# Block maxima of a context taken ahead of its keys and values, and gates loaded later, in the opening stage of a two-layer gated cross-attention kernel

## The chip, the cores and the metric

The kernel runs on one core of one Trainium2 chip. The core has five engines with an instruction queue each: TensorE (PE: matrix products and transposes, with its weight loads shown as PEld), VectorE (DVE), ScalarE (ACT), GpSimd (POOL) and SyncE (SP, which here issues most of the DMA transfers). Each engine takes its instructions strictly in the order of its program, and engines wait for one another through semaphores. The metric is the device time of one execution in microseconds (us), as the median of several runs.

## The reference

Two layers, each a gated cross attention and a gated feed-forward, over `x` of 4 batches of 512 rows of 512 numbers. A context of 4 x 512 x 512 serves both layers.

```python
x = x + tanh(g_xattn[0]) * L0_xattn(layernorm(x), ctx)      # a product of quantized rows and context
x = x + tanh(g_ffn[0])   * L0_ffn(layernorm(x), w1, w2)     # ternary weights, 512 -> 2048 -> 512, gelu twice
x = x + tanh(g_xattn[1]) * L1_xattn(layernorm(x), ctx, ctx, mask, Wq, Wk, Wv, Wo)   # softmax attention
x = x + tanh(g_ffn[1])   * L1_ffn(layernorm(x), ...)        # 8 experts, 2 a row, and shared experts
```

The stage that the change touches is the first line, with the keys and values that line three will need:

```python
def L0_xattn(x, weight):          # weight is the context of one batch
    xq = quant_dequant_act_1x128(x)          # per row and 128 columns: max|x|, round to fp8, scale back
    wq = quant_dequant_weight_128x128(weight)  # per block of 128x128: max|w|, round to fp8, scale back
    return einsum('emk,enk->emn', xq, wq)
K = key @ Wk;  V = value @ Wv     # layer 1, key = value = ctx, not rounded
```

The maximum of a block of the context is taken over 128 x 128 numbers, and keys and values must be made from the context before it is rounded.

## The kernel before, in words

The 2048 rows are 16 tiles of 128 rows (`t` = 0 to 15), four to a batch. Tiles go through layer 0 in a pipeline written out by hand: `step(s)` does the rows of tile `s + 7` (`cross_rows`: normalization, scaling, fp8 rounding), the product of tile `s + 6` with its context (`cross_product`), statistics and normalization for the feed-forward of tiles in between, the first feed-forward product of tile `s` (`hidden`), the scales of tile `s - 1` and the second product of tile `s - 2` (`down`). The steps run from -7 to 14. Within a step a list `between` puts in further pieces: parts of a context, and the sums, means and roundings of the two feed-forward weights w1 and w2.

The context of batch `b` is prepared by a generator, `cross_context(b)` (line 663), of which `go(pieces, n)` runs the next `n` pieces. Before the change the pieces are:

1. the keys (line 669, four products into `k_ps`, copied to SBUF by ACT, line 676);
2. the values (line 681, sixteen small products into `v_ps`, copied by ACT, line 688);
3. the block maxima: `cam` (DVE, line 696) holds the maxima of each partition, a PE transpose into `tpm` (line 700), `cpeak` and `cwide` (DVE, lines 702 and 704), a second transpose (line 705), and from it `csafe` and `cup`, the scale of each block and its inverse (DVE, lines 707 to 711);
4. to 7. one piece for each quarter: scaling by `cup` (DVE, line 715), fp8 rounding (DVE, lines 136 to 141, in `fp8_round`), and scaling back by `csafe` (ACT, line 722, four instructions of 128 columns).

Context 0 is prepared whole ahead of step -7 (`go(cross_context(0), 7)`). Context 1 had keys and values in step -6, maxima and first quarter in step -5, and the rest in step -4, ahead of the product of tile 4, the first that needs it, in step -2. Contexts 2 and 3 are spread in the same way over steps -2 to 0 and 2 to 4.

The rows of tile `t` (`va`) are normalized on DVE (line 130), their maxima `xam` taken (line 734), scaled on ACT (line 741), rounded on DVE (lines 136 to 141) and scaled back on ACT (line 747). `cross_product` transposes them on PE into `tpa` (line 754), copies them with ACT (`vTa`, line 758), multiplies (line 761, `oa`) and adds to `x_sb` on DVE (line 768), times `tg`, the tanh of the gates (line 592). Three buffers hold `va`, so tile `t + 3` waits for the transposes of tile `t`.

The weights w1 and w2 come in four parts of 1 MB. ACT sums the magnitudes of each (`weight_sum`, line 637); then one small PE product `tot_ps` (line 649) adds up over partitions, DVE makes the mean and its inverse `wscale` (lines 650 and 654), and ACT rounds each part (`weight_round`, line 659), after which DVE clips it (line 660). The four buffers of w1's parts are used again for w2, so the transfers of w2 wait for the rounding of w1. The rows of the feed-forward are quantized by ACT with the row scales `nqs` (lines 828 and 846), turned by a DMA transpose into `xqT` and cast by DVE (line 838).

Two things decide the order around the change. PSUM has a pool of two accumulators (`acc`), used in turn by `k_ps`, `v_ps`, `tpm`, `tpa` and `tot_ps`, so that each of these waits until the reader of an earlier one has finished. And the order of each engine's instructions is not that of the source alone: a scheduler orders them by their dependences and by its own estimates when the program is built. The transfers that SP issues are in the order of the source.

Of the kernel before, what the change touches and what calls it, by code (L numbers as in the profile page):

```python
# [10 lines left out]
F32 = mybir.dt.float32  # L11
# [4 lines left out]
AF = mybir.ActivationFunctionType  # L16
ALU = mybir.AluOpType
AX = mybir.AxisListType
PSUM = bass.MemoryType.PSUM

P = 128
# [3 lines left out]
DC = D // P  # L25
# [18 lines left out]
FP8_MAX = 448.0  # L44
# [4 lines left out]
def flamingo_kernel(  # L49
# [22 lines left out]
    nc = tc.nc  # L72

    const = ctx.enter_context(tc.tile_pool(name="const", bufs=1))
    small = ctx.enter_context(tc.tile_pool(name="small", bufs=4))
# [6 lines left out]
    def acc(name):  # L82
        return ps_acc.tile([P, 512], F32, tag="acc", name=name)


    ident = const.tile([P, P], F32, name="ident")
# [12 lines left out]
    gates = const.tile([P, 4], F32, name="gates")  # L99
    tg = const.tile([P, 4], F32, name="tg")  # L100
# [380 lines left out]
    for n in range(last_n + 1):  # L481
        if 0 < n < last_n:
            q = asked(n + 1)
# [75 lines left out]
    with ExitStack() as l0:  # L559
# [9 lines left out]
        with ExitStack() as ph:  # L569
# [17 lines left out]

            load_batch(0)
            load_rows(0)
            nc.sync.dma_start(out=gates[:, 0:2], in_=g_xattn.partition_broadcast(P))  # L590
            nc.sync.dma_start(out=gates[:, 2:4], in_=g_ffn.partition_broadcast(P))
            nc.scalar.activation(tg, gates, AF.Tanh)
            wk_sb = wkv.tile([P, DC, NG * DH], F32, name="wk_sb")
            wv_sb = wkv.tile([P, DC, NG * DH], F32, name="wv_sb")
            nc.sync.dma_start(out=wk_sb, in_=wk.rearrange("(c p) n -> p c n", p=P))
            nc.sync.dma_start(out=wv_sb, in_=wv.rearrange("(c p) n -> p c n", p=P))

            def key_mask():

# [63 lines left out]
            def cross_context(b):  # L663


                c = state["ctx", b]
                k_ps = acc(f"k_ps_{b}")
                for dc in range(DC):
                    nc.tensor.matmul(
                        k_ps,  # L670
                        lhsT=wk_sb[:, dc, :],
                        rhs=c[:, dc, :],
                        start=dc == 0,
                        stop=dc == DC - 1,
                    )
                nc.scalar.copy(kT[:, b, :], k_ps)
                yield
                v_ps = acc(f"v_ps_{b}")
                for kc in range(TB):
                    for dc in range(DC):  # L680
                        nc.tensor.matmul(
                            v_ps[:, kc * P : (kc + 1) * P],
                            lhsT=c[:, dc, kc * P : (kc + 1) * P],
                            rhs=wv_sb[:, dc, :],
                            start=dc == 0,
                            stop=dc == DC - 1,
                        )
                nc.scalar.copy(
                    v_sb[:, b * TB : (b + 1) * TB, :], v_ps.rearrange("p (c n) -> p c n", c=TB)
                )  # L690
                yield
                cb = c.rearrange("p c (n q) -> p (c n) q", q=P)

                am = small.tile([P, 16], F32, tag="cam", name=f"cam_{b}", bufs=2)
                for ns in [slice(4 * dc, 4 * dc + 4) for dc in range(DC)] if b == 0 else [slice(16)]:
                    nc.vector.tensor_reduce(
                        am[:, ns], cb[:, ns, :], AX.X, ALU.max, apply_absolute_value=True
                    )
                tp = acc(f"tpm_{b}")
                nc.tensor.transpose(tp[:16, :P], am, ident)  # L700
                peak = small.tile([16, 1], F32, tag="cpeak", name=f"cpeak_{b}", bufs=2)
                nc.vector.tensor_reduce(peak, tp[:16, :P], AX.X, ALU.max)
                wide = small.tile([16, P], F32, tag="cwide", name=f"cwide_{b}", bufs=2)
                nc.vector.tensor_copy(wide, peak.to_broadcast([16, P]))
                nc.tensor.transpose(tp[:, P : P + 16], wide, ident[:16, :16])
                safe = small.tile([P, 16], F32, tag="csafe", name=f"csafe_{b}", bufs=2)
                nc.vector.tensor_scalar_max(safe, tp[:, P : P + 16], 1e-6)
                up = small.tile([P, 16], F32, tag="cup", name=f"cup_{b}", bufs=2)
                nc.vector.reciprocal(up, safe)
                nc.vector.tensor_scalar_mul(up, up, FP8_MAX)  # L710
                nc.vector.tensor_scalar_mul(safe, safe, 1.0 / FP8_MAX)
                yield
                for dc in range(DC):
                    ns = slice(dc * 4, dc * 4 + 4)
                    nc.vector.tensor_tensor(
                        cb[:, ns, :], cb[:, ns, :], up[:, ns].unsqueeze(2).to_broadcast([P, 4, P]),
                        ALU.mult,
                    )
                    e = apool.tile([P, 512], F32, tag="e", name=f"ce_{b}_{dc}")
                    fp8_round(c[:, dc, :], e)  # L720
                    for n in range(dc * 4, dc * 4 + 4):
                        nc.scalar.mul(cb[:, n, :], cb[:, n, :], safe[:, n : n + 1])
                    yield
# [205 lines left out]
            def go(pieces, n=1):  # L929
                for _ in range(n):  # L930
                    next(pieces, None)
# [29 lines left out]
            with ExitStack() as first:  # L961
                stg = first.enter_context(tc.tile_pool(name="stg", bufs=4))
                ws = (w1T, w2T)
                wd = (w1q, w2q)
                load_batch(1)
                load_rows(1)
                load_weight(stg, 0, ws[0])
                load_batch(2)
                for b in range(2, B):
                    load_rows(b)  # L970
                go(cross_context(0), 7)
                cross_stats(0)

                def w(f, k, *cs):
                    return [lambda c=c: f(k, c, wd[k]) for c in cs]

                ctx1, ctx2 = cross_context(1), cross_context(2)
                step(-7)
                step(-6, [lambda: go(ctx1, 2)] + w(weight_sum, 0, 0, 1))
                step(-5, [lambda: go(ctx1, 2)] + w(weight_sum, 0, 2, 3))  # L980
                weight_mean(0)
                scales_left(0)
                step(-4, [lambda: go(ctx1, 3), lambda: cross_stats(1)] + w(weight_round, 0, 0, 1))
                load_weight(stg, 1, ws[1])
                step(-3, w(weight_round, 0, 2, 3) + w(weight_sum, 1, 0))
                load_batch(3)
                step(-2, [lambda: go(ctx2, 2)] + w(weight_sum, 1, 1, 2, 3))
                weight_mean(1)
                scales_left(1)
                step(-1, [lambda: go(ctx2, 2)] + w(weight_round, 1, 0, 1, 2, 3))  # L990
# [335 lines left out]
    for n in range(2):  # L1326
        m, f = rt(f"m{n}", 1), rt(f"f{n}", 1)
# [70 lines left out]
    go = []  # L1398
# [237 lines left out]
```

## Time and profile before

| what | value |
|---|---|
| median of 3 runs | 1269.71 us (1268.26 to 1270.74) |
| the profiled execution | 1276.27 us, of which the span is 1274.6 us |
| PE, DVE, ACT, POOL busy in the span | 92%, 48%, 40%, 32% |
| granted TensorE clock, mean over the span | 0.969 |
| first 20 us: PE, DVE, ACT busy | 8.12, 13.61, 5.55 us |
| 80 to 100 us: PE, DVE, ACT busy | 15.66, 16.55, 15.02 us |
| 400 to 600 us: PE, DVE, ACT busy | 199.37, 126.19, 100.65 us |
| 900 to 1275 us: PE, DVE, ACT busy | 360.63, 55.15, 61.64 us |

A row of the timeline gives the start, the busy time, the engine, the line of the kernel, the operation, the tiles written and read, and how many instructions are merged; in brackets stands how long the engine stood idle ahead of it, and whose result ended that idle time. A row of the waits gives who waited for whom, the total in us, how often, and the longest. A row of the stretches gives, after the length, the busy time of PE, PEld, DVE, ACT and POOL with the number of instructions, then the granted TensorE clock (1.00 is full), the share of the DMA engines and GB/s. The execution that was profiled is one of its own, slower than the median of the runs by 6.56 us.

### The profile page before, as it was taken

To read this page: it belongs to the slowest core of one execution; us is meant where nothing else is said; L and a number is where in the kernel's file an instruction comes from. 1 tells how busy PE (TensorE), PEld (TensorE's weight loads), DVE (VectorE), ACT (ScalarE), POOL (GpSimd) and SP (SyncE) were. 2 spreads that over 40 slices of the span, in tenths; PEclk is the share of its full clock that TensorE was granted. 3 is DMA by queue.
4 is the path that set the end of the run, shared out by engine and by line. 5 is a ranking of instruction groups with operands and counts; after the bars stand their busy time and mean duration, and the time that the engine had idled before them with its cause. 6 is when DMAs were issued, how large, how long until landed. Compare 5 with 4: busy or idle time off the path is not lost. (4 is left out here: it accounts for less than half of the span.)

```text
span 1274.6 us, 14308 instructions
## 1 busy us (share of the span) xinstructions
PE 1169.5 (92%) x5246; PEld 531.7 (42%) x5262; DVE 607.4 (48%) x1157; ACT 511.3 (40%) x710; POOL 411.5 (32%) x409
## 2 busy tenths in 40 slices
PE   3777797899899999999999999998999999999996
PEld 2333443344233333333333444443335555555553
DVE  7699999788556665655654511321121111111110
ACT  4688897777255555454454111100001121212211
POOL 1000100111267777767787301155000111111111
PEclk8778899999899999999999999998999999999998
DMA  9240222334121111111003000055215886888782
GB/s 341 68 135 13 42 57 47 85 79 109 37 66 35 48 55 35 59 43 60 1 2 141 9 1 1 0 214 192 67 65 174 241 253 192 260 255 250 221 260 34
DMA packets 88752, 135.32 MB, mean 106 GB/s; under 512 B 52836, under 2 KB 54120, under 8 KB 84840
## 3 DMA queue, kind: packets, MB, share of 16 engines
q1 hardware_dynamic: 80936, 116.52, 28.8%
q0 software_dynamic: 7744, 17.86, 6.4%
q8 instruction: 42, 0.69, 0.2%
q14 instruction: 30, 0.25, 0.1%
HBM read 113.84 MB, written 32.32 MB: 115 GB/s over the span
## 5 line engine op out<-in xcount | busy, mean ns | idle before, releaser
L428 ACT ACTIVATE ex<-s,mbias,mk 128x1024 f32<-128x1024 f32 x128 | 147.3, 1201 | 140.4 <-PE s L239 140.4
L319 DVE TENSOR_REDUCE nmax<-s 128x2 f32<-128x1024 f32 x128 | 150.3, 1216 | 98.6 <-PE s L239 87.9
L1475 PE MATMUL gue<-w,xT 128*128 128x352 f32 x576 | 176.3, 459 | 0.0
L1516 POOL DMA_INDIRECT out_dram<-ye,row_i x36 | 55.5, 1542 | 325.7 <-ACT ye L1515 226.3
L389 POOL TENSOR_TENSOR part<-part,ex 128x1024 f32<-128x1024 f32 x62 | 144.6, 2353 | 16.4 <-PE sm L239 11.4
L1219 PE MATMUL gu<-xnT_d,w 128*128 128x512 f32 x320 | 140.3, 593 | 0.7 <-ACT xnT_d L1173 0.7
L1475 PEld LDWEIGHTS gue<-w,xT 128*128 128x128 f32 x576 | 109.1, 190 | 70.4 <-issue 16.9
L1498 DVE COPY hT<-tph_e 128x256 f32<-128x256 f32 x36 | 15.3, 425 | 248.6 <-PE tph_e L1495 248.6
L1506 PE MATMUL oe<-w,hT 128*128 128x512 f32 (+1 forms) x216 | 102.3, 609 | 3.2 <-DVE hT L1498 0.5
L1219 PEld LDWEIGHTS gu<-xnT_d,w 128*128 128x128 f32 x320 | 59.9, 190 | 73.9 <-issue 72.1
L761 PE MATMUL oa<-ctx,vTa 128*128 128x512 f32 x128 | 69.4, 693 | 18.8 <-ACT vTa L758 18.7
L1207 ACT ACTIVATE sg<-gu,sgb 128x512 f32<-128x512 f32 x20 | 13.8, 688 | 176.0 <-PE gu L1219 157.2
L389 POOL TENSOR_TENSOR part<-ex,ex 128x1024 f32<-128x1024 f32 x32 | 75.8, 2393 | 22.7 <-ACT ex L428 22.7
L239 PE MATMUL s<-row_tables 10*128 10x512 bf16 (+1 forms) x512 | 67.3, 383 | 9.2 <-DVE nmax L319 5.7
L1484 ACT ACTIVATE sge<-gue 128x352 f32<-128x352 f32 x35 | 16.3, 466 | 147.3 <-PE gue L1475 147.3
L239 PE MATMUL s<-k,qT 32*128 32x512 f32 x512 | 72.1, 604 | 0.4 <-ACT qT L287 0.4
L912 PE MATMUL ob<-w2q,hqT 128*128 128x512 bf16 x248 | 62.0, 397 | 11.3 <-DVE hqT L838 10.4
L239 PE MATMUL s<-qT,k 32*128 32x512 f32 x512 | 71.4, 598 | 0.0
L239 PE MATMUL av<-ex,kv 128*32 128x512 f32 x512 | 69.2, 605 | 0.4 <-ACT ex L428 0.4
L239 PE MATMUL q_ps<-xnT,wq_sb 128*128 128x512 f32 (+1 forms) x156 | 68.8, 553 | 0.0
L1208 DVE SCALAR_TENSOR_TENSOR hd<-gu,sub,sg 128x512 f32<-128x512 f32 x20 | 15.0, 750 | 111.5 <-ACT sg L1207 105.4
L239 PE MATMUL oc<-wo,attnT 128*128 128x512 f32 (+1 forms) x164 | 66.2, 525 | 0.0
(262 smaller groups left out, 1650.8 us busy)
## 6 DMA issues: line engine op xcount, KB each, us to landing
w<-in_e_w_dram SPq DMA_DIRECT2D x36, 1408.0 KB
w<-in_e_w_dram SPq DMA_DIRECT2D x36, 768.0 KB
slots<-row_tables SPq DMA_DIRECT2D x13, 771.0 KB
xr<-slots SPq DMA_DIRECT2D x36, 256.0 KB
stage<-in_w1T_dram SPq DMA_DIRECT2D x4, 1024.0 KB
stage<-in_w2T_dram SPq DMA_DIRECT2D x4, 1024.0 KB
k<-kv SPq DMA_DIRECT2D x64, 64.0 KB
out_dram<-x_sb SPq DMA_DIRECT2D x16, 256.0 KB
```

The source lines that it names most:

```text
L239: tc.keep_in_program_order(nc.tensor.matmul(*args, **how))
L319: largest = nc.vector.tensor_reduce(nmax[:, i, 2 * j : 2 * j + 2], sc[j], AX.X, ALU.max, negate=True)
L389: nc.gpsimd.tensor_tensor(part[:, hs, :], old[:, hs, :], ex[:, hs, :], ALU.add)
L428: nc.scalar.activation(ex[:, 2 * j : 2 * j + 2, :], sc[j], AF.Exp, bias=mbias[:, b, kc : kc + 1], scale=mk[:, b, kc : kc + 1],)
L761: nc.tensor.matmul(o_ps[:, 0, :], lhsT=vT[:, dc, :], rhs=cq[:, dc, :], start=dc == 0, stop=dc == DC - 1,)
L912: nc.tensor.matmul(o_ps, lhsT=hqT[:, c, :], rhs=w2q[:, c * D : (c + 1) * D], start=c == 0, stop=c == IC - 1,)
L1219: nc.tensor.matmul(gu[:, m, :], lhsT=w[:, dc, c * P : (c + 1) * P], rhs=xnT[:, dc, b * S : (b + 1) * S], start=dc == 0, stop=dc == DC - 1,)
L1475: nc.tensor.matmul(gu[:, m, :I], lhsT=xT[:, dc, :], rhs=wt[:, dc, :], start=dc == 0, stop=dc == DC - 1,)
L1484: nc.scalar.activation(sg, gu[:, 0, :I], AF.Silu)
L1498: nc.vector.tensor_copy(hT[:, :2, :], tp[:, : 2 * P].rearrange("p (c q) -> p c q", q=P))
L1506: nc.tensor.matmul(o_ps[:, 0, :], lhsT=hT[:ni, c, :], rhs=dw[:ni, c, :], start=c == 0, stop=c == len(ICH) - 1,)
L1516: added = nc.gpsimd.indirect_dma_start(out=out, out_offset=bass.IndirectOffsetOnAxis(ap=row_i[:, j, 0:1].bitcast(I32), axis=0), in_=y, in_ ...
```

## The change

Three things move; no operation is added or taken away.

- In `cross_context` the block maxima become the first piece, ahead of the keys and the values. This holds for all four contexts.
- Context 1 has its maxima, keys and values in step -7 and nothing in step -6; one quarter follows in step -5 and three in step -4, as before. The first product, of tile 0, stands in step -6. Contexts 2 and 3 keep their numbers of pieces for each step: context 2 now has maxima and keys in step -2, values and the first quarter in step -1.
- The loads of the two gates and the tanh of them stand after the loads of `wk` and `wv` instead of ahead of them.

```diff
             load_batch(0)
             load_rows(0)
-            nc.sync.dma_start(out=gates[:, 0:2], in_=g_xattn.partition_broadcast(P))
-            nc.sync.dma_start(out=gates[:, 2:4], in_=g_ffn.partition_broadcast(P))
-            nc.scalar.activation(tg, gates, AF.Tanh)
             wk_sb = wkv.tile([P, DC, NG * DH], F32, name="wk_sb")
             wv_sb = wkv.tile([P, DC, NG * DH], F32, name="wv_sb")
             nc.sync.dma_start(out=wk_sb, in_=wk.rearrange("(c p) n -> p c n", p=P))
             nc.sync.dma_start(out=wv_sb, in_=wv.rearrange("(c p) n -> p c n", p=P))
+            nc.sync.dma_start(out=gates[:, 0:2], in_=g_xattn.partition_broadcast(P))
+            nc.sync.dma_start(out=gates[:, 2:4], in_=g_ffn.partition_broadcast(P))
+            nc.scalar.activation(tg, gates, AF.Tanh)
...
                 c = state["ctx", b]
+                cb = c.rearrange("p c (n q) -> p (c n) q", q=P)
+
+                am = small.tile([P, 16], F32, tag="cam", name=f"cam_{b}", bufs=2)
+                for ns in [slice(4 * dc, 4 * dc + 4) for dc in range(DC)] if b == 0 else [slice(16)]:
+                    nc.vector.tensor_reduce(
+                        am[:, ns], cb[:, ns, :], AX.X, ALU.max, apply_absolute_value=True
+                    )
+                tp = acc(f"tpm_{b}")
+                nc.tensor.transpose(tp[:16, :P], am, ident)
+                peak = small.tile([16, 1], F32, tag="cpeak", name=f"cpeak_{b}", bufs=2)
+                nc.vector.tensor_reduce(peak, tp[:16, :P], AX.X, ALU.max)
+                wide = small.tile([16, P], F32, tag="cwide", name=f"cwide_{b}", bufs=2)
+                nc.vector.tensor_copy(wide, peak.to_broadcast([16, P]))
+                nc.tensor.transpose(tp[:, P : P + 16], wide, ident[:16, :16])
+                safe = small.tile([P, 16], F32, tag="csafe", name=f"csafe_{b}", bufs=2)
+                nc.vector.tensor_scalar_max(safe, tp[:, P : P + 16], 1e-6)
+                up = small.tile([P, 16], F32, tag="cup", name=f"cup_{b}", bufs=2)
+                nc.vector.reciprocal(up, safe)
+                nc.vector.tensor_scalar_mul(up, up, FP8_MAX)
+                nc.vector.tensor_scalar_mul(safe, safe, 1.0 / FP8_MAX)
+                yield
                 k_ps = acc(f"k_ps_{b}")
...
                 nc.scalar.copy(
                     v_sb[:, b * TB : (b + 1) * TB, :], v_ps.rearrange("p (c n) -> p c n", c=TB)
                 )
-                yield
-                cb = c.rearrange("p c (n q) -> p (c n) q", q=P)
...
                 yield
                 for dc in range(DC):
                     ns = slice(dc * 4, dc * 4 + 4)
...
                 ctx1, ctx2 = cross_context(1), cross_context(2)
-                step(-7)
-                step(-6, [lambda: go(ctx1, 2)] + w(weight_sum, 0, 0, 1))
-                step(-5, [lambda: go(ctx1, 2)] + w(weight_sum, 0, 2, 3))
+                step(-7, [lambda: go(ctx1, 3)])
+                step(-6, w(weight_sum, 0, 0, 1))
+                step(-5, [lambda: go(ctx1, 1)] + w(weight_sum, 0, 2, 3))
                 weight_mean(0)
                 scales_left(0)
                 step(-4, [lambda: go(ctx1, 3), lambda: cross_stats(1)] + w(weight_round, 0, 0, 1))
```

The removed maxima are the same lines that are added above.

More of the change, by code (lines that the diff above doesn't have):

```diff
@@ L690, in cross_context @@
                 )
-                yield
-                cb = c.rearrange("p c (n q) -> p (c n) q", q=P)
[L694 to L711, printed above, removed]
                 yield
```

## The prediction

> **What bounds the kernel now.** I read the page's busy shares and slices first, then busy time by stretches, then the waits of the vector engine (DVE) in the first 130 us, then the timeline around those waits.
>
> ```profile
> span 1274.6 us, 14308 instructions
> PE 1169.5 (92%) x5246; PEld 531.7 (42%) x5262; DVE 607.4 (48%) x1157; ACT 511.3 (40%) x710; POOL 411.5 (32%) x409
> ...
> PE   3777797899899999999999999998999999999996
> DVE  7699999788556665655654511321121111111110
> ```
> ```profile
> 20.00:40.00 20.00, 4.94 (x26) 3.19 (x25) 19.03 (x46) 15.43 (x34) 1.02 (x1) 0.61 0.79 299
> 40.00:60.00 20.00, 18.37 (x72) 10.52 (x71) 11.30 (x38) 8.86 (x19) 0.00 (x0) 0.93 0.00 1
> 60.00:80.00 20.00, 13.17 (x27) 5.54 (x27) 18.64 (x43) 19.16 (x35) 0.00 (x0) 0.69 0.70 229
> 100.00:130.00 30.00, 21.11 (x69) 9.14 (x69) 29.39 (x62) 24.47 (x46) 2.54 (x3) 0.89 0.05 10
> 130.00:160.00 30.00, 24.71 (x93) 12.86 (x93) 28.80 (x89) 25.19 (x42) 3.75 (x5) 0.83 0.23 45
> 160.00:200.00 40.00, 36.54 (x142) 16.63 (x144) 37.55 (x110) 38.40 (x60) 2.95 (x4) 1.00 0.26 50
> ```
> ```profile
> DVE x_sb L768 <- PE oa L761: 7.7, 4, 2.3
> DVE va L130 <- PE tpa L754: 4.1, 1, 4.1
> ```
> ```profile
> 22.12 0.28 DVE L702 TENSOR_REDUCE cpeak<-tpm 16x1 f32<-16x128 f32 x1 [0.66 <-PE tpm L700]
> 37.37 1.06 PE L754 MATMUL tpa<-ident,va 128*128 128x128 f32 x3 [14.44 <-ACT va L747]
> 46.84 3.73 PE L681 MATMUL v_ps<-wv_sb,ctx 128*128 128x128 f32 x32
> 51.15 0.55 DVE L130 TENSOR_SCALAR va<-x_sb,mv_a,rstd_a 128x512 f32<-128x512 f32 x1 [4.13 <-PE tpa L754]
> 51.74 3.70 PE L761 MATMUL oa<-ctx,vTa 128*128 128x512 f32 x8 [0.21 <-ACT vTa L758]
> 55.48 0.75 DVE L768 SCALAR_TENSOR_TENSOR x_sb<-oa,tg,x_sb 128x512 f32<-128x512 f32 x1 [2.30 <-PE oa L761]
> 55.53 0.38 PE L649 MATMUL tot_ps<-wtot,ones 128*128 128x1 f32 x2
> 57.59 5.79 ACT L659 ACTIVATE w1q<-stage,wscale 128x2048 int16<-128x2048 f32 x3
> 57.75 5.40 PE L761 MATMUL oa<-ctx,vTa 128*128 128x512 f32 x8 [0.73 <-ACT vTa L758]
> 97.73 0.75 DVE L768 SCALAR_TENSOR_TENSOR x_sb<-oa,tg,x_sb 128x512 f32<-128x512 f32 x1 [2.02 <-PE oa L761]
> ```
>
> From about 255 us TensorE (PE) is the bound: nine tenths or more in nearly every slice. The change lies wholly ahead of that, so it moves the end only by moving the start of that stretch. In the stretch rows (PE, PEld, DVE, ACT, POOL busy; granted clock; DMA) DVE works 19.03 of 20 us, then 11.30 of 20, then again 18.64 of 20 and 95.74 of 100 up to 200 us. So DVE is nearly the bound for 200 us, with one hole, 40 to 60, where PE is full (18.37) after an idle stretch of its own (4.94). The timeline tells why. PE waits 14.44 us for the first scaled rows (`va`), and then the products of tiles 0 and 1 and the second context's keys and values reach it all at once; DVE waits for PE 2.0, 4.13 and 2.30 us, and the sum `tot_ps`, which ACT's weight rounding needs, runs only at 55.53.
>
> **Part 1: context maxima ahead, second context's keys and values in PE's hole.** The work is the same, instruction for instruction; its order changes on PE, DVE and ACT until about 190 us. I walk the changed kernel's order with the durations of the rows above and around them (start to start on DVE: 0.60 for a 128x512 add, reduction or statistic, 0.34 for a scalar form, 2.20 for the 128x2048 maxima; on ACT 0.30 per 128x128 scaling, 1.81 per 128x2048; on PE 3.5 for k, 3.73 for v, 3.6 for a warm product).
>
> DVE starts rounding context 0 at 23.68 now. Ahead of it go 3.1 us of statistics of batch 1, which move behind, and the waits 0.66 (row 22.12) and 0.25 (for the second transpose): 19.7 in the changed order. Rounding takes 9.9 us (23.68 to 33.59), so it ends near 29.6. PE meanwhile ends context 0's values near 22.0 as now (row L688 starts 22.01) and goes on to context 1's keys, done at 25.7. Its values need ACT's copy of those keys, which stands behind eight scalings of context 0 (2.44): 28.0. After five of 16 value blocks PE waits again, for `cwide`, which DVE makes behind the rounding: 31.0. The values end at 33.8, where now they end at 50.6. `va` of tile 0 is scaled at 33.7 and copied (`vTa`) at 36.6, after one weight sum and the copy of the values; product 0 runs 36.6 to 40.2 (now 41.69 to 45.3), product 1 41.5 to 45.1 (now from 51.74), `tot_ps` at 45.2, and the first rounding of w1 at 47.5 against 57.59, 10.1 earlier. Going on, the row scales `nqs` of batch 0 come near 79 against 91.56, with 2.3 us of DVE work (tile 6's rounding 1.9, small ones 0.4) not yet done that is done now: about 10 us gained.
>
> The sum by DVE's idle time says the same and shows what is uncertain. What goes: 0.66 + 0.25, 2.03 (product 0's add at 45.33), 4.13, 2.30, 1.36 (product 2's add at 63.19) and 2.02 (product 5's at 97.73), together 12.75 us. What is late next:
> - The products 0 to 2 follow gaps of 1.3 to 2.2 us in the walk. A product took 3.60 to 3.70 us after dense work (51.74) and 5.40 after gaps (57.75), 1.8 more. All at full rate: DVE waits nothing. All slow: 0.7, 2.5 and 2.2 us at their adds, 5.4. The gaps resemble those ahead of 57.75 about as much as those ahead of 51.74, so I take half, 2.7.
> - `csafe` of context 1 follows its transpose with little between: 0.2 to 0.6 (now 0.25 at 22.97); 0.6.
> - The cast of the first transposed rows (`xqT`) stands about 4 us after `nqs` in DVE's new order. Row quantization 0.71 and the transpose come between; the nearest row is the hidden transpose (ACT ends 228.68, cast waits until 233.09: 4.4). So 0 to 1.5; 1.3.
> - Product 5's add stands further back in the order: 0 to 2.02 left; 0.75.
> - Context 3, near 140 us: product 8 now stands after the first of four key steps, three key steps (2.6) ahead of the values; ACT's copy of the values stands ahead of `hq` of tile 1. In that stretch DVE is 96% busy, ACT 84%: 0 to 2.7; 1.0.
> Sum: -12.75 + 2.7 + 0.6 + 1.3 + 0.75 + 1.0 = -6.4 us. With each at its good end -12.55, at its bad end -12.75 + 5.4 + 0.6 + 1.5 + 2.02 + 2.7 = -0.5.
>
> The first of these turns on the clock. Granted clock is 0.61 in 20 to 40, where PE idles 14.4 us, and 0.93 in 40 to 60. The Trainium skill, "TensorE: Matmul & The Clock Gate", Part 1, says that PE falls to half rate after about one idle window of 3.4 us and needs about as much sustained work to recover. It speaks against taking the filler from between the products; yet the gaps between products in the walk are under such a window, so by the rule alone the products stay fast and the sum is -9.1 (1260.6); the 5.40 row, after gaps under 2 us, does not bear that out, by the rows it is -6.4.
>
> **Part 2: gates later.** SP issues the same six transfers ahead of context 1, which still goes out at 7.71. The two weight loads move up by the gates' two slots (4.57 to 5.68), up to 1.1 us for PE's first key step at 11.88. The gates land behind 512 KB more: 11.14 plus up to 1.7 at the 305 GB/s of that stretch. ACT's table load (1.28) and tanh (0.20) end by 14.4; ACT's first real work is at 15.94 now, 15.6 in the walk. Cost nothing, covered by DVE's first row scales; if the gates land after about 14.1, every us of that delays ACT. An earlier `wk` gains 0 to 0.3, since the first key step now stands ahead of the second transpose. I count 0.
>
> **The time.** The profiled execution took 1276.27 us (span 1274.6), 6.56 over the median of the runs, 1269.71. 1276.27 - 6.4 = 1269.9 against itself; from the median, 1263.3.
>
> **Rivals.**
> 1. The products stay fast. For it: 3.60 and 3.70 at 41.69 and 51.74, and gaps of at most 2.2 us between them in the walk; this is what the skill's rule above makes of it. Against: 5.40 at 57.75 after gaps no longer. -6.4 - 2.7 = -9.1: 1260.6.
> 2. All three products slow, PE's work being thinner. For it: clock 0.61 and 0.69 in two stretches, 5.40 at 57.75. Against: the 14.44 us hole itself goes. -6.4 + 2.7 = -3.7: 1266.0.
> 3. The front gets ahead but the lead is given back by 200 us: all bad ends together, -0.5: 1269.2. For it: DVE is 96% busy there, so no stall is made up. Against: the totals of work are the same and start earlier.
> 4. Slower. ACT's queue is blocked near 140 us at its copy of context 3's values: PE has product 8 and three key steps ahead of them, behind the second transpose, which waits for DVE's `cwide`; behind the copy wait `hq` of tile 1, row quantization 4 and hidden tile 3. In the walk `cwide` is made 6.9 us after the maxima of hidden tile 1 begin (125.91 now); product 8 now starts 12.3 us after them, so 5.4 are in hand. The price is 2.7 plus all that `cwide` is later than those 12.3. In place of the 1.0 in the sum it gives -7.4 plus the price, so it decides from a price of 9.9 (slower by 2.5); with a whole period of hidden tiles lost (158.51 to 170.69, and so on: 11.6 on average) it ends at +4.2: 1273.9. For it: PE waits longest there for such a chain (3.12 for `vTa` at 138.19). Against: the 5.4 in hand.
> 5. The order does not do what it says, since context 1 lands after 17.4 and DVE stands at its maxima. They start at 16.59 now without waiting, so I give this nothing of its own.
>
> **How the numbers follow.** Forecast 0.40, rival 1 0.20, rival 2 0.15, rival 3 0.11, rival 4 0.14. 0.2% is 2.5 us, about what a measurement of this kernel can tell from no change. Faster 0.40 + 0.20 + 0.15 = 0.75, same 0.11, slower 0.14. The likeliest time is 1263.3. The range goes from 1257.2 (-12.55, all good ends) to 1270.5 (rival 3 and the 0.1% that the runs shown differ by); it leaves out rival 4 and a little at each end.
>
> **What would show it.** In the changed profile: DVE's rounding of context 0 from about 19.7; PE idle ahead of `tpa` (14.44) gone and granted clock above 0.61 in 20 to 40; `v_ps` of context 1 done near 34; `tot_ps` near 45 to 49 and the first rounding of w1 near 47 to 51; DVE above 16 busy of 20 in 40 to 60; PE's full stretch starting some 6 us earlier. I am wrong if the products at 36 to 56 take 5.4 and DVE waits behind each, if the lead at 92 us is gone at 200, or if ACT stands at the copy of context 3's values for more than 5 us.

## The result, and the profile after

The changed kernel takes 1256.45 us (median of 5 runs, 1256.43 to 1256.96) against 1270.48 (5 runs, 1268.26 to 1270.74): a ratio of 0.9897, 95% interval 0.9886 to 0.9908, so some 13 us faster (11.7 to 14.5 on 1270.48); the two medians lie 14.0 us apart. The profiled execution took 1256.45 us itself (span 1254.8). The forecast had the direction and half of the size, and the time lies 0.75 us below its range.

The page of the changed kernel: span, busy totals, and the slices of PE and DVE.

```profile
span 1254.8 us, 14322 instructions
PE 1163.9 (93%) x5262; PEld 531.2 (42%) x5262; DVE 606.4 (48%) x1157; ACT 510.8 (41%) x710; POOL 412.7 (33%) x409
...
PE   5776988899899999999999999999999999999996
DVE  7999999787457666656654511331221111111110
```

DVE's total is the same within 1.0 us (606.4 against 607.4); it is packed into less time. Its stretches (length; PE, PEld, DVE, ACT, POOL busy; granted clock; DMA):

```profile
20.00:40.00 20.00, 14.05 (x58) 9.60 (x57) 20.00 (x48) 17.35 (x41) 0.00 (x0) 0.83 0.78 295
40.00:60.00 20.00, 14.59 (x40) 6.75 (x39) 19.58 (x50) 17.61 (x33) 1.39 (x1) 0.91 0.39 127
60.00:80.00 20.00, 11.67 (x29) 5.12 (x28) 18.79 (x59) 14.18 (x28) 2.69 (x2) 0.74 0.38 135
```

The hole is filled: DVE works 20.00 and 19.58 of 20 us where it worked 19.03 and 11.30, and PE in 20 to 40 works 14.05 instead of 4.94. In the waits of the first 130 us DVE's 7.7 us for products and 4.1 us for `tpa` have become

```profile
DVE x_sb L768 <- PE oa L761: 1.7, 3, 0.8
DVE ctx L715 <- PE v_ps L702: 0.9, 1, 0.9
```

and the timeline shows, row by row, what answers the rows of before (maxima are now L671 to L686, values L702):

```profile
19.89 1.29 DVE L715 TENSOR_TENSOR ctx<-ctx,cup 128x512 f32<-128x512 f32 x2 [0.88 <-PE v_ps L702]
30.93 0.28 PE L680 MATMUL tpm<-ident,cwide 16*128 16x16 f32 x1 [2.22 <-DVE cwide L679]
31.15 4.97 PE L702 MATMUL v_ps<-wv_sb,ctx 128*128 128x128 f32 x22
35.95 0.60 PE L754 MATMUL tpa<-ident,va 128*128 128x128 f32 x4
37.13 0.54 DVE L130 TENSOR_SCALAR va<-x_sb,mv_a,rstd_a 128x512 f32<-128x512 f32 x1
37.28 3.70 PE L761 MATMUL oa<-ctx,vTa 128*128 128x512 f32 x8 [0.73 <-ACT vTa L758]
42.09 3.70 PE L761 MATMUL oa<-ctx,vTa 128*128 128x512 f32 x8 [0.67 <-ACT vTa L758]
45.63 0.28 PE L649 MATMUL tot_ps<-wtot,ones 128*128 128x1 f32 x2
45.83 0.75 DVE L768 SCALAR_TENSOR_TENSOR x_sb<-oa,tg,x_sb 128x512 f32<-128x512 f32 x1 [0.32 <-PE oa L761]
47.13 3.70 PE L761 MATMUL oa<-ctx,vTa 128*128 128x512 f32 x8 [0.73 <-ACT vTa L758]
47.35 2.00 ACT L659 ACTIVATE w1q<-stage,wscale 128x2048 int16<-128x2048 f32 x1 [0.27 <-DVE wout L778]
86.03 0.73 DVE L768 SCALAR_TENSOR_TENSOR x_sb<-oa,tg,x_sb 128x512 f32<-128x512 f32 x1
```

`tpa` no longer waits 14.44 us, the three products behind it all take 3.70, `tot_ps` comes at 45.63 instead of 55.53 and the first rounding of w1 at 47.35 instead of 57.59. Up to tile 0 the adds of the products wait 0.32 us in all (product 1); product 5's (row 86.03) waits for nothing.

**Where the lead arises and whether it stays.** The second gelu of each hidden tile (L877 on ACT) is a mark that every kernel here has. That of tile 0 starts at 98.22 us instead of 108.34, of tile 5 at 169.78 instead of 181.99, of tile 9 at 223.30 instead of 235.30, of tile 15 at 289.41 instead of 301.63; the first maxima of the attention (L319) come at 263.24 instead of 275.49, the first matmul of L1219 at 698.88 instead of 710.94. So 10.1 us are there at tile 0, 12.0 at tile 9, and 12 stay. (The profiled run of before lies 6 us above its median because of a stall at 867 us, which the last section tells. Without it the run would come out near 1268.5 us, 2 us under the median, by an estimate from the figures there; that is as much as the medians' 14.0 exceed the 12.0 of these marks.)

DVE's account up to tiles 0 and 9, kernel before:

```profile
0.00:108.34 108.34, 63.47 (x221) 34.02 (x222) 87.45 (x229) 72.33 (x140) 7.77 (x25) 0.83 0.47 163
0.00:235.30 235.30, 172.08 (x627) 84.81 (x636) 205.56 (x551) 180.39 (x311) 19.80 (x40) 0.89 0.34 98
```

and the changed kernel:

```profile
0.00:98.22 98.22, 61.42 (x222) 34.47 (x222) 89.65 (x239) 72.25 (x140) 9.71 (x26) 0.87 0.51 180
0.00:223.30 223.30, 168.18 (x636) 84.69 (x636) 204.16 (x551) 179.88 (x311) 21.02 (x40) 0.92 0.35 104
```

Up to tile 9 DVE has the same 551 instructions, 205.56 and 204.16 us of them. What differs is its idle time, length minus busy: 20.89 us up to tile 0 and 29.74 up to tile 9 before, 8.57 and 19.14 after. That is the measure by which the experiments are read.

### The profile page after: what moved, and what is told of

The parts are those of the page before. It is cut to its first block, busy times and chain, and to the rows that moved or that the text cites. A ratio compares the mean times of both kernels' runs of the same rounds, so it can differ in the third digit from the quotient of the medians.

```text
span 1254.8 us, 14322 instructions
## 1 busy us (share of the span) xinstructions
PE 1163.9 (93%) x5262; PEld 531.2 (42%) x5262; DVE 606.4 (48%) x1157; ACT 510.8 (41%) x710; POOL 412.7 (33%) x409
## 5 line engine op out<-in xcount | busy, mean ns | idle before, releaser
L319 DVE TENSOR_REDUCE nmax<-s 128x2 f32<-128x1024 f32 x128 | 150.3, 1215 | 98.8 <-PE s L239 88.0
L1475 PE MATMUL gue<-w,xT 128*128 128x352 f32 x576 | 176.3, 459 | 0.0
L1219 PE MATMUL gu<-xnT_d,w 128*128 128x512 f32 x320 | 140.4, 593 | 0.7 <-ACT xnT_d L1173 0.7
L1475 PEld LDWEIGHTS gue<-w,xT 128*128 128x128 f32 x576 | 109.1, 190 | 70.4 <-issue 16.9
L1219 PEld LDWEIGHTS gu<-xnT_d,w 128*128 128x128 f32 x320 | 59.9, 190 | 73.9 <-issue 72.1
L1207 ACT ACTIVATE sg<-gu,sgb 128x512 f32<-128x512 f32 x20 | 13.7, 687 | 176.8 <-PE gu L1219 176.8
L761 PE MATMUL oa<-ctx,vTa 128*128 128x512 f32 x128 | 65.9, 662 | 19.1 <-ACT vTa L758 19.1
```

The lines of the kernel that those rows point to most:

```text
L319: largest = nc.vector.tensor_reduce(nmax[:, i, 2 * j : 2 * j + 2], sc[j], AX.X, ALU.max, negate=True)
L761: nc.tensor.matmul(o_ps[:, 0, :], lhsT=vT[:, dc, :], rhs=cq[:, dc, :], start=dc == 0, stop=dc == DC - 1,)
L1219: nc.tensor.matmul(gu[:, m, :], lhsT=w[:, dc, c * P : (c + 1) * P], rhs=xnT[:, dc, b * S : (b + 1) * S], start=dc == 0, stop=dc == DC - 1,)
L1475: nc.tensor.matmul(gu[:, m, :I], lhsT=xT[:, dc, :], rhs=wt[:, dc, :], start=dc == 0, stop=dc == DC - 1,)
```

## Experiments

Each was compared with the kernel before on the same chip. The kernel before took 1269.5 us on the chip of the first four and 1277 on those of the others (the last section tells where the difference lies), so ratios are compared, not times. Steps, pieces and names are those of the section on the kernel before.

**The parts alone, and all but one.** First the gates alone, loaded behind `wk` and `wv` in the kernel before.

```diff
-            nc.sync.dma_start(out=gates[:, 0:2], ...)   # and [:, 2:4], and the tanh
             nc.sync.dma_start(out=wk_sb, ...)
             nc.sync.dma_start(out=wv_sb, ...)
+            nc.sync.dma_start(out=gates[:, 0:2], ...)   # and [:, 2:4], and the tanh
```

> The kernel before with the gates' loads and the tanh behind the loads of wk and wv, and nothing else. My theory (the second context's keys and values, moved into the hole in which PE waited 14.44 us for the first scaled rows, make the gain, the rest little): within 1 us of the kernel before. Rival (the earlier wk lets PE begin 1.2 us sooner and this carries through): 1 to 2 us faster. The first key step should start near 10.7 instead of 11.88 and ACT's table load end about 1 us later, both without any follow-up at 57 us, where w1 is first rounded.

Measured: 1269.32 us, ratio 0.9999 (0.9987 to 1.0011). The first key step starts at 10.75 instead of 11.88, as expected. Tile 0 comes 1.2 us earlier, tile 9 2.0 us later. Alone, the gates are worth nothing; but the order of DVE and ACT is another here too, so this run doesn't show the load by itself.

Then the keys and values of context 1 alone, a step earlier, with the old order of pieces:

```diff
-                step(-7)
-                step(-6, [lambda: go(ctx1, 2)] + w(weight_sum, 0, 0, 1))
+                step(-7, [lambda: go(ctx1, 2)])
+                step(-6, w(weight_sum, 0, 0, 1))
```

> The kernel before with keys and values of context 1 in step -7 instead of -6; the block maxima stay behind keys and values, the gates where they were. My theory: most of the gain is here, 7 to 10 us faster (1260 to 1263), with the first rounding of w1 near 50 instead of 57.59; what is missing to the changed kernel is DVE's start of context 0's rounding, which stays near 23.7. Rival (the maxima ahead do it, since DVE is nearly the bound for 200 us and its work starts 3.8 us sooner): at most 3 us faster.

Measured: 1262.66 us, ratio 0.9946 (0.9920 to 0.9972). That is some 6.9 us, at the low edge of the theory and more than the rival's 3. Tile 0 comes 7.8 us earlier, tile 9 5.3.

Then the new order of the pieces (maxima first) with the old steps and gates:

```diff
+                am = small.tile(...)        # the maxima, up to `safe`
+                ...
+                yield
                 k_ps = acc(f"k_ps_{b}")
```

> The changed kernel's order of pieces (block maxima ahead of keys and values, in all four contexts), with the steps and the gates of the kernel before: context 1 has maxima and keys in step -6, values and the first quarter in step -5. My theory: 2 to 4 us faster than before (1266 to 1268), DVE's rounding of context 0 from about 20, but product 1 and the sum of w1 still late. Rival (the maxima ahead do it): 9 us faster or more.

Measured: 1270.87 us, ratio 1.0012 (1.0002 to 1.0021). Tile 0 comes 5.1 us earlier, tile 4 6.0, and then the lead is lost: tile 5 0.35 us later than before, tile 9 2.9. Neither expectation came true in the total.

Last, the whole change but for the gates, which stay ahead of `wk`:

```diff
+            nc.sync.dma_start(out=gates[:, 0:2], ...)   # and [:, 2:4], and the tanh
             nc.sync.dma_start(out=wk_sb, ...)
             nc.sync.dma_start(out=wv_sb, ...)
-            nc.sync.dma_start(out=gates[:, 0:2], ...)   # and [:, 2:4], and the tanh
```

> The changed kernel with the gates' loads and the tanh back ahead of wk and wv. My theory: within 1 us of the changed kernel, so 13 to 14 us faster than the kernel before. Rival (the gates' part matters): 1 to 2 us slower than the changed kernel, with the first key step back at 11.9.

Measured: 1267.48 us, ratio 0.9983 (0.9974 to 0.9993): 11 us slower than the changed kernel. My theory, that the gates cost nothing, fell, and the rival's 1 to 2 us were too little as well. Up to tile 9 of this kernel:

```profile
0.00:101.14 101.14, 65.12 (x221) 35.53 (x222) 88.40 (x231) 71.87 (x140) 8.02 (x25) 0.86 0.51 174
0.00:233.23 233.23, 173.20 (x627) 87.19 (x636) 204.41 (x551) 180.50 (x311) 19.70 (x40) 0.89 0.34 99
```

DVE's work is again 204.41; its idle time is 12.74 up to tile 0 and 28.82 up to tile 9. The scheduler had ordered the same work differently on PE, DVE and ACT: context 1's values, for instance, stand whole ahead of the second transpose of its maxima, where the changed kernel has them on both sides of it. On the chip the first product then ran at 36.04 in 6.59 us instead of 3.70, with DVE's adds waiting 4.3 us for products up to tile 0, and tile 5 fell 8.4 us behind.

**Load or order?** Two kernels separate them. In one the gates' loads stand between the two weights; the order of PE, DVE, ACT and POOL is exactly that of the changed kernel.

```diff
             nc.sync.dma_start(out=wk_sb, ...)
+            nc.sync.dma_start(out=gates[:, 0:2], ...)   # and [:, 2:4]
             nc.sync.dma_start(out=wv_sb, ...)
-            nc.sync.dma_start(out=gates[:, 0:2], ...)   # and [:, 2:4]
```

> The changed kernel with the gates' two loads between those of wk and wv instead of behind both (the tanh stays where it was). The order of the instructions on PE, DVE, ACT and POOL is exactly that of the changed kernel; only SP's queue differs. Theory (the order decides): wv lands some 0.5 us later, nothing else, so 1256 to 1258 us (ratio to the kernel before 0.989 to 0.990), second gelu of tile 0 near 98.2 us, of tile 5 near 170. Rival (the gates' loads themselves cost, by holding up a weight of context 0's keys and values): about half of what their place ahead of both weights cost, 1260 to 1263 us (ratio 0.993 to 0.995).

In the other the gates stay last and only the two weights change places; PE's and DVE's order is then exactly that of the 1267.48 us kernel.

```diff
-            nc.sync.dma_start(out=wk_sb, ...)
             nc.sync.dma_start(out=wv_sb, ...)
+            nc.sync.dma_start(out=wk_sb, ...)
```

> The changed kernel with the load of wk behind that of wv; the gates stay last. On PE and DVE the order is exactly that of the run with the gates ahead of wk (1267.48 us), on ACT but for the place of a few lines, while the gates are loaded as late as in the changed kernel. Theory (the order decides): 1266 to 1269 us (ratio 0.997 to 0.999), with the second gelu of tile 5 some 8 us behind the changed kernel's (near 178 us), ACT waiting 3 us and more for the last quarters of context 3 near 165 us. Rival (the gates' loads cost): 1256 to 1258 us, tile 5 near 170 us.

Measured: gates between 0.9894 (0.9875 to 0.9913; 1263.52 us), as the changed kernel; `wv` first 0.9988 (0.9978 to 0.9997; 1275.32 us), as the kernel with the gates ahead. Tile 5 comes at 169.32 and at 176.10. So it is the order that decides, in both. What the gates' load itself costs in front of `wk` is less well known: with `wv` first all marks are 1.8 to 2.1 us earlier than with the gates first, but kernels of equal order up to there came 0.4 to 1.7 us apart at tile 0 from one chip to another. On one chip, the kernel with the gates ahead and context 3 early (below), whose order on PE and DVE is the same up to tile 3, lies 1.0 us behind `wv` first at tiles 0 to 3, in one profile of each. Why the scheduler orders differently for so small an edit stays open.

**What is lost where.** With the gates ahead of `wk` most goes between tiles 4 and 5 (18.56 us, 13.05 in the changed kernel). ACT's queue there:

```profile
162.81 1.28 ACT L747 ACTIVATE va<-va,xam 128x128 f32<-128x128 f32 x4 [1.28 <-DVE va L141]
164.35 1.28 ACT L722 ACTIVATE ctx<-ctx,csafe 128x128 f32<-128x128 f32 x4 [0.26 <-DVE ctx L141]
168.94 1.28 ACT L722 ACTIVATE ctx<-ctx,csafe 128x128 f32<-128x128 f32 x4 [3.31 <-DVE ctx L141]
```

Behind these scalings of context 3 stands `hq` (L902), whose transposed result PE needs; PE then waits 6.30 us:

```profile
177.24 1.89 PE L912 MATMUL ob<-w2q,hqT 128*128 128x512 bf16 x4 [6.30 <-DVE hqT L838]
```

In the changed kernel DVE has rounded context 3 by then, ACT scales two quarters at once without a wait, and PE's wait (at 169.44) is 1.49:

```profile
159.42 2.46 ACT L722 ACTIVATE ctx<-ctx,csafe 128x128 f32<-128x128 f32 x8
```

Three kernels move one more quarter of context 3 from step 4 into step 3, so that ACT finds less to wait for; the orders are unchanged up to that quarter.

```diff
-            step(3, [lambda: go(ctx3, 2)])
-            step(4, [lambda: go(ctx3, 2), lambda: cross_stats(3)])
+            step(3, [lambda: go(ctx3, 3)])
+            step(4, [lambda: go(ctx3, 1), lambda: cross_stats(3)])
```

In the kernel with the gates ahead of `wk`:

> The run with the gates ahead of wk, and one more quarter of context 3's rounding in step 3 instead of step 4 (three and one instead of two and two). Up to that quarter the orders of DVE, PE and ACT are exactly those of the run that took 1267.48 us. Theory (the loss in step 4 is ACT standing behind the last quarters of context 3, 1.3 + 0.3 + 3.3 us of waits, and PE 6.3 us behind it): those waits fall to under 1.5 us together, tile 5's second gelu comes near 173 to 175 us instead of 178.2, and the time is 1262 to 1265 us (ratio 0.993 to 0.996). Rival (the two steps together hold too much work for DVE, and where the quarter stands is all the same): the wait moves to step 3, tile 5 near 178 us, 1266 to 1269 us.

Measured: ratio 0.9956 (0.9941 to 0.9971; 1271.71 us) instead of 0.9983. The waits of ACT shrink from 4.85 to 1.12 us,

```profile
162.26 1.28 ACT L747 ACTIVATE va<-va,xam 128x128 f32<-128x128 f32 x4 [0.59 <-DVE va L141]
164.07 1.28 ACT L722 ACTIVATE ctx<-ctx,csafe 128x128 f32<-128x128 f32 x4 [0.53 <-DVE ctx L141]
```

PE's from 6.30 to 0.98, tile 5 comes at 173.73 instead of 178.15, and 4.4 us are still there at tile 15 (0.9 of them were there at tile 0 already). The theory of this wait held.

In the kernel with maxima first, which lost its lead at the same place:

> The run with the new order of the pieces, but the old steps and gates (ratio 1.0012), and one more quarter of context 3's rounding in step 3 instead of step 4. Theory (it lost its lead in step 4, where ACT waited 1.48 and 2.58 us for DVE and PE then 7.55 us for the turned hidden tile): those waits shrink to under 2 and under 4 us, tile 5's second gelu comes 4 to 7 us earlier (175.5 to 178.5 us instead of 182.3), ratio 0.995 to 0.998. Rival (the lead was lost for another reason): tile 5 within 2 us of 182.3 us, ratio 0.9995 to 1.002.

Measured: ratio 1.0003 (0.9993 to 1.0013; 1278.10 us) instead of 1.0012. Tile 5 came at 178.59 instead of 182.34, a little less than expected, but 2 of the 3.75 us were there at tile 3 already, and from tile 8 on nothing is left beyond them. PE's wait fell from 7.55 to 2.46 us, yet ACT now waits 2.24 us for `va` at 168.00 and 1.76 at 182.28. Here my theory was right about PE's wait and wrong about the lead, and the ratio is the rival's: ACT waits for DVE at the next place instead. That DVE was late as a whole is my reading of these rows; no run tests it.

In the changed kernel, as a counter-test:

> The changed kernel with the same quarter of context 3 in step 3 instead of step 4. Theory: in the changed kernel ACT doesn't wait there, so nothing is gained: tile 5's second gelu within 1.5 us of the changed kernel's 169.8 us, ratio 0.989 to 0.991. Rival (the earlier quarter is worth 4 us by itself, as it was behind the gates ahead of wk): tile 5 near 165.5 us, ratio 0.986 to 0.987.

Measured: ratio 0.9895 (0.9879 to 0.9912; 1264.46 us): nothing gained, as ACT has no wait there to lose. Tile 5 came at 171.92, a little outside what was expected; 1.7 of these 2.1 us were there at tile 0.

**The cost of context 1's keys and values in their old place.** The kernel before without them (POOL fills both with zeros: these products are left out, and the rest goes on with zeros):

```diff
+                if b != 1:
                     k_ps = acc(f"k_ps_{b}")   # keys, and further down the values
                     ...
+                else:
+                    nc.gpsimd.memset(kT[:, b, :], 0.0)   # and v_sb
```

> The kernel before without the keys and values of context 1 (POOL fills them with zeros, so the output is another). Theory (in the kernel before they stand on the path, at the cost of the front's delay): second gelu of tile 0 comes 7 to 10 us earlier (98.5 to 101.5 us instead of 108.3), as when they are only moved into PE's idle time (-7.8), and the time falls to 1258 to 1264 us, not much below the 1262.7 us of moving them. Rival (the lead comes from elsewhere, such as the maxima): tile 0 no more than 5.5 us earlier (what PE takes for them), time over 1265 us.

Measured: 1302.91 us, ratio 1.0180 (1.0140 to 1.0220); this total says nothing of the front, and I should have foreseen it: with other values the tokens are routed otherwise, and the experts' part issues 624 matmuls of the form that was 576 before. The marks ahead of it can be read: tile 0 at 101.39, 7.0 us earlier (at the low edge of the 7 to 10 expected, above the rival's 5.5), tile 5 5.6. That is about what moving them gave (7.8 and 7.0), so in the hole they cost next to nothing. In their old place PE worked 9.2 us on them between 38.23 and 50.57 (5.50 on the keys, 3.73 on the values), and 7.0 of these reached tile 0.

**The other two contexts.** The changed kernel with the old order of pieces for contexts 2 and 3:

```diff
-                # in words: maxima, keys, values, in this order for every context
+                for piece in (peaks, to_keys, to_values) if b < 2 else (to_keys, to_values, peaks):
```

> The changed kernel, but contexts 2 and 3 keep the old order of the pieces (keys and values ahead of the block maxima). Up to the rounding of w1's last quarter, near 60 us, the order of all engines is that of the changed kernel. Theory (the front gives 10 us, contexts 2 and 3 the other 2 us between 100 and 160 us): tile 0's second gelu within 1 us of the changed kernel's (97.5 to 99.5 us), tile 5's 1 to 4 us behind it, time 1257 to 1261 us if the kernel before has 1270 (ratio 0.990 to 0.993). Rival (contexts 2 and 3 do nothing of their own; only the front counts): tile 5 within 0.5 us, ratio 0.989 to 0.990.

Measured: ratio 0.9927 (0.9910 to 0.9943; 1268.03 us), 0.0030 or some 4 us worse than the changed kernel, which was measured on another chip; 3.6 us worse than the changed kernel with context 3 early (above), on the same chip. Tile 0 is the same (97.85); it falls 1.5 us behind at tile 1, 2.6 at tile 3 and 4.1 at tile 9. The order of pieces of contexts 2 and 3 thus is worth some 4 us by itself (at tile 9 only 2.1 against the kernel on the same chip), which no term of the forecast had.

And the changed kernel with context 2's maxima, keys and values all in step -3:

```diff
-                step(-3, w(weight_round, 0, 2, 3) + w(weight_sum, 1, 0))
+                step(-3, [lambda: go(ctx2, 3)] + w(weight_round, 0, 2, 3) + w(weight_sum, 1, 0))
...
-                step(-2, [lambda: go(ctx2, 2)] + w(weight_sum, 1, 1, 2, 3))
+                step(-2, w(weight_sum, 1, 1, 2, 3))
...
-                step(-1, [lambda: go(ctx2, 2)] + w(weight_round, 1, 0, 1, 2, 3))
+                step(-1, [lambda: go(ctx2, 1)] + w(weight_round, 1, 0, 1, 2, 3))
```

> The changed kernel, with the maxima, keys and values of context 2 in step -3 and one quarter of its rounding left in step -1 (three in step 0). Theory (what pays is fp32 work of PE in PE's idle time ahead of a product that waits for DVE): between 55 and 75 us PE has idle time in the changed kernel, so tile 0's second gelu comes 0 to 3 us earlier (95 to 98 us), ratio 0.987 to 0.990. Rival (DVE is the engine that has no room there, and context 2's maxima now stand ahead of the rounding of w1): tile 0 later by 1 to 4 us (99 to 102 us), ratio 0.990 to 0.993.

Measured: ratio 0.9926 (0.9910 to 0.9943; 1267.92 us). Each expectation was half right: tile 0 is 2.0 us earlier than in the changed kernel, as the theory said, and the ratio is the rival's, since the lead is lost by tile 5 (2.7 us late) and tile 9 (4.2). No version here beats the changed kernel.

**All runs in one account.** Times in us; idle is length minus DVE's busy time in the view shown above, and the last column is the idle time between tiles 0 and 9. The kernel without context 1's keys and values is left out, as its work is another.

| kernel | ratio | tile 9 | DVE busy to tile 9 | DVE idle to tile 0 | tile 0 to 9 |
|---|---|---|---|---|---|
| before | 1 | 235.30 | 205.56 | 20.89 | 8.86 |
| gates alone | 0.9999 | 237.34 | 205.34 | 19.79 | 12.21 |
| keys and values of 1 early | 0.9946 | 229.96 | 205.21 | 11.75 | 13.00 |
| maxima first | 1.0012 | 238.16 | 204.92 | 14.70 | 18.54 |
| maxima first, context 3 early | 1.0003 | 236.02 | 205.09 | 13.34 | 17.59 |
| all but gates | 0.9983 | 233.23 | 204.41 | 12.74 | 16.08 |
| `wv` first | 0.9988 | 231.28 | 204.17 | 10.95 | 16.16 |
| all but gates, context 3 early | 0.9956 | 228.81 | 203.83 | 11.86 | 13.12 |
| context 2 early | 0.9926 | 227.53 | 204.00 | 10.17 | 13.36 |
| old order for 2 and 3 | 0.9927 | 227.41 | 204.35 | 9.26 | 13.80 |
| changed, context 3 early | 0.9895 | 225.30 | 204.01 | 10.24 | 11.05 |
| changed | 0.9897 | 223.30 | 204.16 | 8.57 | 10.57 |
| gates between | 0.9894 | 222.96 | 204.08 | 8.23 | 10.65 |

DVE's work is 203.8 to 205.6 us in all of them; its idle time runs from 18.9 to 33.2 us. Since tile 9 is the sum of the two, it follows the idle time, and the ratios follow tile 9 within 3.5 us. This account says where a lead is kept or lost, not yet why; the why rests on the experiments above. The front gives 6 to 13 us in every version but that with the gates alone; what is left of it is decided between tiles 0 and 9, where the kernel before, with 8.86 us, is the best of all and the changed kernel close to it.

## Why the prediction was right in direction and half the size

**The walk** of the changed order held. Rounding of context 0 starts at 19.89 (said 19.7), product 0 at 37.28 (36.6), product 1 at 42.09 (41.5), `tot_ps` 45.63 (45.2), w1's rounding 47.35 (47.5), `nqs` 78.05 (79, against 91.56). Only context 1's values end late, at 36.1 instead of 33.8: the last 11 of their 16 products (22 instructions) took 4.97 us, at a granted clock of 0.50 (from 29.06 to 35.89), where all 32 instructions had taken 3.73 before.

**What goes, 12.75 us,** held: of the seven waits only 0.32 us at product 1's add is left, and DVE's idle time up to tile 0 fell by 12.32.

**What is late next, 6.35 us,** is the step that failed. In front of tile 0 I had put 5.35: 2.7 for products at the slow clock, 0.6 for `csafe`, 1.3 for the cast of `xqT`, 0.75 for product 5. Since 12.32 of 12.75 were gained there, 0.43 came: 0.88 where DVE waits for PE's products for context 0's values (row 19.89, which the walk didn't have) and 0.32 at product 1, less 0.77 by which the other waits (for DMA and POOL, and the smallest) got shorter. Products 0 to 2 took 3.70 each, as the granted clock was 1.00 from 35.89 to 56.37, and their adds waited 0.32 together; `csafe` (31.41), the cast and product 5's add waited for nothing. I had charged each term with its middle or its bad end.

The charges were not absurd: in the order of the kernel with the gates ahead, DVE waits 1.51 us for `csafe` and 4.3 at the adds of products, and product 0 takes 6.59 us because the clock is 0.50 from 35.08 to 41.91. So they hang on the order: in all five profiles that have the changed kernel's order up to there, products 0 to 2 took 3.70 each, and in the three with the other order product 0 took 5.40 to 6.59. In the changed kernel context 1's values keep PE at work without a gap from 32.48 to 35.89, and at 35.89 the clock comes back; with the gates ahead they end at 32.6, PE works about 2.1 of the 3.4 us up to 35.08, and the clock falls. No step of the walk had this. That small waits are not independent, since each that does occur lets the next operand arrive, is my reading; no run tests it. For the products the Trainium skill's "TensorE: Matmul & The Clock Gate", Part 1 (half rate after about one idle window of 3.4 us), gave 1260.6, nearer than my halving of the 5.40 row. That row shows less than I read from it: the clock fell at 58.58, 0.83 us after product 2 of the kernel before had begun (last section).

**Context 3, 1.0 us:** ACT waited 0.94 at the copy of its values (136.91), 6.07 at 133.02 for row scales and nothing at the scalings. Between tiles 0 and 9 DVE's idle time is 1.71 us longer than before, and up to tile 9 its busy time is 1.40 us shorter: together +0.3. How much of the 1.71 is context 3's isn't separated.

**The sum** by these sizes: -12.32 + 1.71 - 1.40 = -12.0, which is tile 9's lead. The measured ratio gives -13.1 (-11.7 to -14.5), so no gain is missing beyond what the measurement can tell; the all-good-ends sum of -12.55 was the nearest, and the range ended 0.75 us short because its low end was taken from it without anything for what a ratio of two kernels leaves uncertain.

**Gates later, "I count 0".** As a load this held within about 1 us (0.9894 when put between the weights, with the same order; some 1.0 us slower at tile 0 when put ahead of both, against `wv` first); as a part of the change it did not, since without it the scheduler's order is another and 11 us are gone. The forecast was right here only because it walked the order that the whole change makes. I had costed parts as if they added; alone they give -7, +1.5 and 0 us, together -13.

**The rivals.** 1 (products stay fast) came true as a mechanism, though its 1260.6 kept the other charges. 2 (products slow) is wrong here and half true in a sibling: with the gates ahead of `wk` product 0 took 6.59 us, though the others of the first three took 3.70. 3 (lead given back by 200 us) is wrong here and exactly what the version with maxima first did, by 8.8 us between tiles 4 and 9. 4 (ACT blocked near 140 us) is wrong at its place, 0.94 us; the same kind of block struck at 165 us in the siblings, at the scalings of context 3 instead of the copy. 5 had nothing to it: context 1's maxima start at 16.44 on time.

**What would show it:** the signs named came: rounding from 19.89, clock 0.83 in 20 to 40, DVE 19.58 in 40 to 60, w1's rounding at 47.35. Context 1's values were done 2 us later than said, and PE's full stretch starts 12 us earlier, not 6.

## What to carry to other kernels

Where one engine is busy nine tenths for a long stretch, count its idle time over the whole stretch, for every version: its work hardly changed here, and the idle time is what differed. Take the waits that a fuller queue might bring as a bound, not as a sum of middles: here they came to 1.2 us in one order of the same work and to some 6 in another. And look for what is lost further on, because a lead in front is kept only if the next steps add no idle time. Where a scheduler orders the instructions, the parts of a change don't add: compare the built orders first, and separate an edit's own cost from that of the order with a kernel that has the one without the other.

## What the runs showed that I had not expected

A product of eight matmuls took 3.60 to 3.70 us at full clock and 4.5 to 6.6 otherwise, and the wait ahead of it doesn't tell which. After a wait of 4.00 us it was slow in the changed kernel (55.27, 5.40 us), as the Trainium skill's "TensorE: Matmul & The Clock Gate", Part 1, has it. But in the kernel with the gates ahead and context 3 early it was slow after 2.02 us, behind dense work, where the changed kernel's after 1.74 us was fast; and 57.75 of the kernel before was slow after 0.73:

```profile
201.63 3.70 PE L761 MATMUL oa<-ctx,vTa 128*128 128x512 f32 x8 [1.74 <-ACT vTa L758]
```
```profile
159.91 5.40 PE L761 MATMUL oa<-ctx,vTa 128*128 128x512 f32 x8 [2.02 <-ACT vTa L758]
```

The granted clock tells them apart. These are stretches of the kernel before and of the kernel with the gates ahead and context 3 early:

```profile
58.58:62.00 3.42, 3.42 (x5) 1.35 (x4) 3.24 (x8) 3.42 (x3) 0.00 (x0) 0.50 0.30 74
```
```profile
160.30:163.71 3.41, 3.41 (x5) 1.33 (x4) 3.41 (x8) 2.65 (x5) 0.00 (x0) 0.50 0.00 0
```

Just ahead of them and just behind them it is 1.00, so both products had begun when it fell. In all fourteen profiles the clock is 1.00 or 0.50, and all its changes lie whole multiples of 3.41 us apart. In the first 330 us of these profiles a step of 3.41 us at full clock in which PE was busy for less than 0.40 of it was always followed by 0.50; the clock came back only after a step with 0.83 or more. Between 0.40 and 0.65 it fell or stayed. In the step ahead of 58.58 PE was busy 2.23 us of 3.41 (0.65), ahead of 160.30 1.39 (0.41); what decides between these two shares stays open.

The three groups of experiments ran on three chips, and the kernel before took 1269.52, 1276.97 and 1277.50 us on them. The difference lies in one place that the change doesn't touch. From the first matmul of L1475 to the end every profile here takes 313.5 us, but for the kernel without context 1's keys and values. From the first matmul of L1219 to the first of L1475 the changed kernel and the one with the gates ahead take 242.36 us; the profiled run of before takes 250.12, 7.8 us more, and the kernel with the gates between 249.95. In the profiles of the second and third group PE stands still once there, for 5.3 to 5.6 us ahead of L1255 (5.44 at 854.20 with the gates between), as it does for 5.48 us at 866.88 in the profiled run of before, which is why that run was 6 us over its median; in the first group's profiles and the changed kernel's it doesn't. Behind it the granted clock is 0.50 for a while (up to 858.02 with the gates between), which makes up most of the rest. With the gates between, PE waits there for DVE's add (L1262), DVE for ACT (L1207, `sg_h`), and ACT starts that instruction only at 852.01, although its product was done at 843.42; in the changed kernel ACT starts it as the product ends, at 844.09. The profile puts ACT's wait down to something outside the core ("remote"); what that is stays open.
